# Two-layer recurrent attention kernel: attend spread over four 64x64 tiles, q's feature rows reordered, last transposes one expert later

## The chip, the core and the metric

The kernel runs on one core of one Trainium2 chip. A core has five engines that run in parallel, each with its own queue of instructions in a fixed order: TensorE (PE; its weight loads are shown as PEld), VectorE (DVE), ScalarE (ACT), GpSimd (POOL) and SyncE (SP, which here only issues DMAs). An instruction at the head of a queue that has to wait holds everything behind it on that engine. The metric is the device time of one execution in microseconds; lower is better.

## What is computed

Two layers of attention multiplied by a gated feed-forward network, on `x` of 4 x 512 x 128 in float32. The change is in the first attention and in the feature rows of the second. The first attention (16 heads, key and value width 64, segments of 64 tokens, a memory carried from segment to segment) is, cut to what matters:

```python
scores = einsum('bhid,bhjd->bhij', q, k) * scale        # own keys, causal mask
att_dot = einsum('bhij,bhjv->bhiv', softmax(scores), v)
sq = elu(q) + 1;  sk = elu(k) + 1
att_mem = sq @ M / (sq @ Z.T)
M_new = M + einsum('bhld,bhlv->bhdv', sk, v);  Z_new = Z + sk.sum(-2)
att = gate * att_mem + (1 - gate) * att_dot              # gate = sigmoid(betas)
out = att.reshape(B, 64, H * DV) @ Wo
```

The result `x + out * silu(ffn(xn))` is normalised and goes through a second attention (16 heads of width 8, 16 channels, softmax over 512 keys) and a second network of 8 experts. The second attention is computed through features: a product of pairs of elements of q gives part of the softmax's denominators.

## The kernel before, in words

**Stages.** The order of the program is: layer norm and the first network (0 to about 92 us of the profile, `norm_ffn0`), the first attention (`attn0`, 92 to 354), the experts of the second network (`ffn1`, about 349 to 490), and the second attention (`attn1`, 490 to the end). Nearly all instructions go through helpers that pin them in the order in which they are written (`mm1` L311 for matmuls, `act1` L314 for ScalarE, `dma1` L323 for SP's DMAs), so the lines of the profile are often those of helpers and the tiles' names tell what an instruction is. Memsets, POOL's products of the first attention and its loads are not pinned; a scheduler puts them where their inputs are ready.

**First attention.** `attn0` works through 32 segments n, 8 for each of 4 batches. A segment has 16 heads, laid out as 4 x 2 x 2 by hp, a and p: head number 4*hp + 2*a + p. Matmuls use 64x64 corners of PE: the rows of a corner are set by the half of the partitions (0 to 63 or 64 to 127, `halves`) in which the operands lie, its columns by the half in which the result lies. In the loop L816 to L856, segment n does in this order on PE: `scores(n+1)` (tile sc), chunks of the projection of a later group (pp for q and k, pv for v; `todo`, three a segment), with `memory(n)` (mm: queries on the memory) and `update(n)` (mu: new memory) between them, `keys(n+1)` (pk: transposes of the keys), then `attend(n)` (dot: softmax weights on the values), in whose middle the transposes of `attended(n-1)` (pa) stand. Every fourth segment brings `output` (po: product with Wo). A dictionary `between` adds steps of the second network's normalisation to segments 18 to 24 and 30.5.

Each step leaves through other engines. VectorE: E from sc (L636), elu (L659), the division of mm and dot (L696, L697), the sum into the memory mz (L733), sums of keys (L664), and rd and sums0 for dot (L755, L757). ScalarE: exponentials (elu, up, E), copies out of PSUM (pj, vt, sk, attT). POOL: t1 by the gate (L714), t2 by one minus the gate (L762), their sum (L763), which pa then transposes. PSUM has three buffers of two banks (`wide`: sc, mm, mu, dot, po) and two of one bank (`narrow`: pp, pv, pk, pa), each used in turn.

In `memory` before the change, the result of head (hp, a, p) lies in half a; in `attend` too, and its operands E and v lie in half a as well (their partitions are the keys, and for keys the half is a). So a group of attend has only corners with equal row and column half. Its two turns go over hp in {0, 1} and {2, 3}, the turn with the transposes between. `attended` moves four transposes to the tile attT with one ScalarE copy of 128x512.

**The gate.** `load_first` loads betas with four DMAs on POOL's queue (L147) into `gate`, laid out as the result of attend is: half a, then hp, p. These come before POOL's setup of the first network in `begin0` (pick at L332 to L341, parts at L347).

**Experts.** `ffn1` goes over batches b and experts e: `up(b, e)` (ph, ScalarE's gelu h), then what `between` holds for (b, e), then `down` of the expert before (eo, added up on VectorE, L957 and L959). `left` holds what the first attention has left: `attended(31)` and `output(7)`. `begin` allocates and fills the second attention's tiles (memsets on POOL, L1150 and L1154) and makes the list of preparations, of which eleven follow from step 13 on.

**Second attention.** `attn1` goes over 64 steps i, 16 for each batch (t = i % 16): each step has 24 matmuls into acc from three functions of the scores, four score matmuls s, two steps ahead, and one preparation or mixing step. ScalarE makes two of the three functions and VectorE the third (L1548). The work for the next batch is spread over t by `prepare1`: tokens k at t = 0 (POOL: tokk, feat, L1207 to L1210), k and q at t = 2 and 3 (POOL splits them into three bf16 parts, L1254 and L1257; SP stores the parts into kd and qd, and q into qe and qf), feature sums pl at t = 4, 7, 9, 11. Every fourth step, `operands1` loads the next group's k and q from kd and qd. `features1` loads the rows of the features (6 DMAs rows from qe, 10 other from qf), and its two `products` multiply rows by other on POOL (L1321). There is one tile `rows` for each half mm of the heads and one tile `other` for both. `bank1` reads the products at t = 8 and 15. The step in which a load is issued and those in which its products stand are the numbers of the table L1617 to L1623.

Of the kernel before, what the change touches and what calls it, by code (L numbers as in the profile page):

```python
# [95 lines left out]
class Kernel:  # L96
# [9 lines left out]
    def load_first(self, pool, pool_attn):  # L106
# [37 lines left out]
        for p in range(2):  # L144
            for a in range(2):

                nc.gpsimd.dma_start(  # L147
                    out=self.gate[a * 64 : a * 64 + 64, :, p, :],
                    in_=be[a, p].partition_broadcast(64),
                )  # L150
# [392 lines left out]
    def attn0(self, xnT, g0, stack, psum, between):  # L543
# [155 lines left out]
        def memory(n):  # L699

            mz, sq = self.mz[(n % 8 + 1) % 2 + 1 if n % 8 else 0], seg[n][0]
            ps = wide(f"mm{n}")
            for hp in range(4):
                for p in range(2):
                    for a in range(2):
                        self.mm1(
                            ps[halves[a], p, hp * (DK + 1) : (hp + 1) * (DK + 1)],
                            lhsT=sq[halves[p], 2 * hp + a, :], rhs=mz[halves[p], hp, a, :],
                            start=True, stop=True,
                        )  # L710
            t = seg[n]["t1"] = pool.tile([P, 4, 2, DK], F32, name=f"t1{n}", tag="t1")
            r = pool.tile([P, 2, 4], F32, name=f"rm{n}", tag="rm")
            divided(ps, t.rearrange("p hp y d -> p y hp d"), r, heads(ps)[:, :, :, DK])
            nc.gpsimd.tensor_mul(t, t, self.gate)  # L714
# [22 lines left out]
        def attend(n, between):  # L737
# [4 lines left out]
            for turn in range(2):  # L742
                for hp in range(2):
                    for p in range(2):
                        for a in range(2):
                            bank, at = (turn + a) % 2, (hp * 2 + p) * (DK + 1)
                            self.mm1(
                                ps[halves[a], bank, at : at + DK + 1],
                                lhsT=e[halves[a], p, bank * 2 + hp, :],
                                rhs=v[halves[a], bank * 2 + hp, p, :], start=True, stop=True,  # L750
                            )
                if turn == 0:
                    between()
# [12 lines left out]
        def attended(n):  # L766

            if n % 4 == 0:

                attT[n // 4] = pool.tile([P, 16, 4, 32], F32, name=f"attT{n}", tag="attT")  # L770
            ps = narrow(f"pa{n}").rearrange("p (hp c) -> p hp c", hp=4)
            for hp in range(4):
                self.pin(nc.tensor.transpose(
                    ps[:, hp, :], seg[n]["att"][:, hp].rearrange("i p v -> i (p v)"),
                    self.ident,
                ))
            self.act1(
                attT[n // 4][:, :, n % 4],
                ps.rearrange("p hp (x c) -> p c (hp x)", c=16), AF.Copy,
            )  # L780
# [35 lines left out]
        for n in range(nseg):  # L816
# [33 lines left out]
            if more and n:  # L850
# [3 lines left out]
            attend(n, (lambda: attended(n - 1)) if n else (lambda: keys(1)))  # L854
# [704 lines left out]
    def attn1(self, xnT, g1):  # L1559
# [4 lines left out]
        with tc.tile_pool(name="a1", bufs=2) as self.a1, tc.tile_pool(  # L1564
# [44 lines left out]
            n = B * 16  # L1609
# [5 lines left out]
            for fb in range(B):  # L1615
                at = fb * 16
                for mm, load, make in (  # L1617
                    (0, at - 7 if fb else 1, at - 4 if fb else 3),
                    (1, at + (1 if fb else 5), at + (6 if fb else 8)),
                ):  # L1620
                    loads.setdefault(load, []).append((fb, mm))
                    for half in range(2):
                        makes.setdefault(make + half, []).append((fb, mm, half))  # L1623
# [342 lines left out]
    def run(self):  # L1966
# [15 lines left out]
        with tc.tile_pool(name="wf1", bufs=1) as wf1, tc.tile_pool(name="f1", bufs=1) as f1:  # L1982
            stack = ExitStack()
            w0 = stack.enter_context(tc.tile_pool(name="w0", bufs=1))
            with tc.tile_pool(name="wf0", bufs=1) as wf0:
                self.load_first(wf0, w0)
# [3 lines left out]
            with tc.tile_pool(name="ap", bufs=1, space=PSUM) as psum:  # L1990
# [23 lines left out]
                def prepare():  # L2014
# [5 lines left out]
                    (0, 1): [(left[0],)], (0, 2): [(left[1],), (begin,)], (0, 3): [(first.sums, 2)],  # L2020
# [77 lines left out]
```

## Time and profile before

| what | value |
|---|---|
| median of 3 runs | 818.4 us (818.02 to 820.14) |
| the profiled execution | 816.52 us, of which the span of the trace is 814.8 us |
| PE busy | 770.7 us (95%) |
| VectorE busy | 594.9 us (73%) |
| ScalarE busy | 505.7 us (62%) |
| POOL busy | 406.9 us (50%) |
| granted clock of PE, mean | 0.985 |

Times in the profile are microseconds from the start of the span, except that the mean of one instruction is in nanoseconds. A group is given as line, engine, operation, result <- inputs with their shapes, count; then busy time and mean; then the idle time of the engine before these instructions and what ended it. A float32 matmul leaves two records, so the 16 x 32 matmuls of attend stand as x1024. In a timeline the bracket at the end of a line is idle time of the engine ahead of it and the instruction that ended it. Busy times of one group are the time in which at least one of its instructions runs, so matmuls that overlap are not counted twice.

### The profile page before, as it was taken

Reading aid. Unit: us, or ns where it says so; the run is one execution under the profiler, and the core shown is the slowest. Engines: PE = TensorE matmul, PEld = TensorE weight load, DVE = VectorE, ACT = ScalarE, POOL = GpSimd, SP = SyncE. Lnnn points to the kernel's source line nnn. Section 1 sums busy time; section 2 is a strip of 40 time slices with the busy share of each in tenths; the row PEclk is TensorE's granted clock in tenths of the full one; section 3 lists DMA queues with packets and bytes.
Section 4 is the critical chain, followed back from the end, with each engine's and each line's share of the span. In section 5 each row is a group of like instructions: output and inputs, shape, how many; then the busy total and the mean of one; then the engine's idle time right before and its main releaser. Section 6 shows DMA issues by size and latency. Waiting matters only on the chain. (4 is left out here: it accounts for less than half of the span.)

```text
span 814.8 us, 23068 instructions
## 1 busy us (share of the span) xinstructions
PE 770.7 (95%) x9708; PEld 452.6 (56%) x9708; DVE 594.9 (73%) x1126; ACT 505.7 (62%) x692; POOL 406.9 (50%) x430
## 2 busy tenths in 40 slices
PE   8999899999999999789999999994999999999996
PEld 4566578787787777666777773331334333422325
DVE  7774687877779779825443338894998999898784
ACT  4333576766767657434432249993897889799760
POOL 7850055646555435545051006937697489624321
PEclk9999999999999999999999999997999999999999
DMA  8700522312313121000015003252344135322000
GB/s 216 170 16 1 155 64 61 93 41 81 92 29 93 29 80 29 16 2 1 1 39 182 1 1 104 87 174 84 107 160 123 41 111 162 105 59 65 1 15 17
DMA packets 74478, 59.21 MB, mean 73 GB/s; under 512 B 41264, under 2 KB 66128, under 8 KB 72928
## 3 DMA queue, kind: packets, MB, share of 16 engines
q1 hardware_dynamic: 72176, 56.25, 23.5%
q0 software_dynamic: 1616, 1.16, 0.9%
q8 instruction: 78, 1.28, 0.7%
q10 hardware_dynamic: 576, 0.26, 0.1%
q14 instruction: 32, 0.26, 0.1%
HBM read 36.41 MB, written 20.97 MB: 70 GB/s over the span
## 5 line engine op out<-in xcount | busy, mean ns | idle before, releaser
L1548 DVE TENSOR_TENSOR e<-e,e 128x1024 f32<-128x1024 f32 x126 | 200.9, 1633 | 15.1 <-ACT e L314 14.8
L311 PE MATMUL acc<-e,strip 128*32 128x512 f32 x1520 | 186.3, 599 | 1.6 <-DVE e L1548 1.5
L314 ACT ACTIVATE e<-s 128x1024 f32<-128x1024 f32 x126 | 122.5, 1029 | 47.9 <-PE s L311 47.6
L314 ACT ACTIVATE e<-e 128x1024 f32<-128x1024 f32 x126 | 127.0, 1070 | 0.0
L311 PEld LDWEIGHTS acc<-e,strip 128*32 128x32 f32 x1520 | 45.9, 109 | 117.2 <-issue 95.1
L314 ACT ACTIVATE h<-ph 128x1024 f32<-128x1024 f32 x32 | 32.8, 1024 | 87.0 <-PE ph L311 87.0
L1321 POOL TENSOR_TENSOR rows<-rows,other 128x512 f32<-128x512 f32 x32 | 62.6, 1985 | 25.1 <-DMA other<-qf 18.1
L659 DVE SCALAR_TENSOR_TENSOR elu<-elu,up 128x512 f32<-128x512 f32 x60 | 68.2, 1137 | 8.5 <-ACT up L314 8.4
L762 POOL TENSOR_TENSOR t<-t,gate 128x512 f32<-128x512 f32 x32 | 40.8, 1275 | 57.3 <-DVE t L697 45.7
L959 DVE SCALAR_TENSOR_TENSOR g<-eo,gw,g 128x128 f32<-128x128 f32 x112 | 31.5, 344 | 49.5 <-PE eo L311 49.5
L311 PEld LDWEIGHTS eo<-w_out,h 128*128 128x128 f32 x512 | 60.9, 192 | 11.7 <-issue 10.4
L314 ACT ACTIVATE pj<-pp 128x512 f32<-128x512 f32 x64 | 38.1, 596 | 44.2 <-PE pp L311 43.8
L311 PE MATMUL eo<-w_out,h 128*128 128x128 f32 x512 | 63.2, 277 | 1.0 <-DVE g L959 0.8
L311 PE MATMUL ph<-xnT,w_in 128*128 128x512 f32 x128 | 61.0, 599 | 0.0
L714 POOL TENSOR_TENSOR t<-t,gate 128x512 f32<-128x512 f32 x32 | 41.2, 1287 | 26.2 <-DVE t L697 26.2
L311 PE MATMUL s<-q,k 64*128 64x512 bf16 x256 | 39.2, 385 | 12.0 <-DMA q<-qd 10.7
L763 POOL TENSOR_TENSOR t<-t,t 128x512 f32<-128x512 f32 x32 | 45.8, 1430 | 2.5
L1207 POOL COPY tokk<-tokk 128x512 f32<-128x512 f32 x4 | 2.4, 610 | 88.8 <-DVE tokk L1196 88.8
L311 PE MATMUL dot<-vone,E 64*64 64x65 f32 x1024 | 44.8, 227 | 0.0
L311 PEld LDWEIGHTS <-k 64*128 64x128 bf16 x256 | 7.4, 94 | 64.9 <-issue 50.0
L311 PEld LDWEIGHTS dot<-vone,E 64*64 64x64 f32 x1024 | 35.8, 137 | 12.2 <-issue 10.9
L314 ACT ACTIVATE elu<-pj 128x512 f32<-128x512 f32 x60 | 37.3, 622 | 0.1
(277 smaller groups left out, 1475.3 us busy)
## 6 DMA issues: line engine op xcount, KB each, us to landing
vd<-vt SPq DMA_DIRECT2D x32, 256.0 KB
vone<-vd SPq DMA_DIRECT2D x64, 128.0 KB
rows<-qe SPq DMA_DIRECT2D x48, 128.0 KB
other<-qf SPq DMA_DIRECT2D x80, 64.0 KB
k<-kd SPq DMA_DIRECT2D x16, 256.0 KB
q<-qd SPq DMA_DIRECT2D x16, 256.0 KB
kd<-partk SPq DMA_DIRECT2D x12, 256.0 KB
qd<-partq SPq DMA_DIRECT2D x12, 256.0 KB
```

The lines of the kernel that those rows point to most:

```text
L311: return self.pin(self.nc.tensor.matmul(*args, **kw))
L314: return self.pin(self.nc.scalar.activation(*args, **kw))
L659: self.vec1(nc.vector.scalar_tensor_tensor(t, t, 1.0, up, ALU.min, ALU.add))
L714: nc.gpsimd.tensor_mul(t, t, self.gate)
L762: nc.gpsimd.tensor_mul(t, t, gate2)
L763: nc.gpsimd.tensor_add(t, t, seg[n]["t1"])
L959: self.vec1(v.scalar_tensor_tensor(acc[b][:, k, :], eo[:, k, :], w, acc[b][:, k, :], ALU.mult, ALU.add))
L1207: self.pool1(nc.gpsimd.tensor_copy(twice[:, :, D1 : 2 * D1], t))
L1321: self.pool1(nc.gpsimd.tensor_mul(rows[:, r], rows[:, r], other[:, r]))
L1548: self.vec1(self.nc.vector.tensor_mul(t, src[0][pair], src[1][pair]))
```

## The change

Five things are changed.

1. `memory` and `attend` write the result of head (hp, a, p) to half (a + hp) % 2, that is crossed for odd hp. In attend, a group of four matmuls now has all four corners, and the bank of a result is a, its row half. The result's place within the bank changes with it (2*u + p in attend, 2*a + hp // 2 in memory, in units of 65). The outputs are stored in the same shapes as before.
2. The gate's layout follows: eight DMAs of half the size in place of four (`crossed`). The fallback branch loads with `crossed` false, also by eight DMAs.
3. `attended` puts its transposes behind all of attend's matmuls, and copies them by four ScalarE copies of 128x128 in place of one of 128x512, since each pair (h, a) goes to other columns of attT. For segment 1, `keys` stands ahead of attend too.
4. In the second attention, the rows for mm = 0 of a batch after the first are loaded at step 16*b - 5 (was - 7) and multiplied at - 2 and - 1 (were - 4 and - 3); for the first batch both halves of mm = 0 are multiplied at step 3 (were 3 and 4), and those of mm = 1 are loaded at 4 (was 5) and multiplied at 6 and 7 (were 8 and 9).
5. In the experts of batch 0, `sums` of batch 2 comes at expert 1 (was 3), `attended(31)` at 2 (was 1), `output(7)` and `begin` at 3 (were at 2).

On SP, by the two programs' orders, the second feature loads of the first batch now stand before the stores of qe, qf and qd, and the loads of k and q at step 10 before the next batch's feature loads. On POOL, all four products of mm = 0 stand before the parts of k.

```diff
-    def load_first(self, pool, pool_attn):
+    def load_first(self, pool, pool_attn, crossed=False):
...
-                nc.gpsimd.dma_start(
-                    out=self.gate[a * 64 : a * 64 + 64, :, p, :],
-                    in_=be[a, p].partition_broadcast(64),
-                )
+                for x in range(2):
+                    rows, cols = (a, slice(x, 4, 2))
+                    if crossed:
+                        rows, cols = (a + x) % 2, slice(2 * a, 2 * a + 2)
+                    nc.gpsimd.dma_start(
+                        out=self.gate[rows * 64 : rows * 64 + 64, cols, p, :],
+                        in_=be[a, p, x:4:2].partition_broadcast(64),
+                    )
...
                     for a in range(2):
+                        at = (2 * a + hp // 2) * (DK + 1)
                         self.mm1(
-                            ps[halves[a], p, hp * (DK + 1) : (hp + 1) * (DK + 1)],
+                            ps[halves[(a + hp) % 2], p, at : at + DK + 1],
                             lhsT=sq[halves[p], 2 * hp + a, :], rhs=mz[halves[p], hp, a, :],
...
-        def attend(n, between):
+        def attend(n):
...
-            for turn in range(2):
-                for hp in range(2):
-                    for p in range(2):
+            for u in range(2):
+                for p in range(2):
+                    for hp in (2 * u, 2 * u + 1):
                         for a in range(2):
-                            bank, at = (turn + a) % 2, (hp * 2 + p) * (DK + 1)
+                            at = (2 * u + p) * (DK + 1)
                             self.mm1(
-                                ps[halves[a], bank, at : at + DK + 1],
-                                lhsT=e[halves[a], p, bank * 2 + hp, :],
-                                rhs=v[halves[a], bank * 2 + hp, p, :], start=True, stop=True,
+                                ps[halves[(a + hp) % 2], a, at : at + DK + 1],
+                                lhsT=e[halves[a], p, hp, :], rhs=v[halves[a], hp, p, :],
+                                start=True, stop=True,
                             )
-                if turn == 0:
-                    between()
...
-            self.act1(
-                attT[n // 4][:, :, n % 4],
-                ps.rearrange("p hp (x c) -> p c (hp x)", c=16), AF.Copy,
-            )
+            src = ps.rearrange("p (a u) (h t c) -> p c a u h t", a=2, h=2, c=16)
+            dst = attT[n // 4][:, :, n % 4].rearrange("p c (u y t) -> p c u y t", u=2, y=4)
+            for h in range(2):
+                for a in range(2):
+                    self.act1(dst[:, :, :, (a + h) % 2 * 2 + a], src[:, :, a, :, h], AF.Copy)
...
-            if more and n:
+            if more:
                 keys(n + 1)
...
-            attend(n, (lambda: attended(n - 1)) if n else (lambda: keys(1)))
+            attend(n)
+            if n:
+                attended(n - 1)
...
-                    (0, at - 7 if fb else 1, at - 4 if fb else 3),
-                    (1, at + (1 if fb else 5), at + (6 if fb else 8)),
+                    (0, at - 5 if fb else 1, (at - 2, at - 1) if fb else (3, 3)),
+                    (1, at + (1 if fb else 4), (at + 6, at + 7)),
                 ):
                     loads.setdefault(load, []).append((fb, mm))
                     for half in range(2):
-                        makes.setdefault(make + half, []).append((fb, mm, half))
+                        makes.setdefault(make[half], []).append((fb, mm, half))
...
-                self.load_first(wf0, w0)
+                self.load_first(wf0, w0, True)
...
-                    (0, 1): [(left[0],)], (0, 2): [(left[1],), (begin,)], (0, 3): [(first.sums, 2)],
+                    (0, 1): [(first.sums, 2)], (0, 2): [(left[0],)], (0, 3): [(left[1],), (begin,)],
```

## The prediction

> **What bounds the kernel now.** I read the busy time by stretches first, then the groups of instructions, then timelines of the places found. Columns of the stretches: length, busy us of each engine with its instructions, granted clock, DMA.
>
> ```profile
> core 0: us, PE busy (x) PEld busy (x) DVE busy (x) ACT busy (x) POOL busy (x), PEclk, DMA share, GB/s
> 100.00:250.00 150.00, 149.26 (x3426) 118.18 (x3424) 115.25 (x231) 101.60 (x183) 82.61 (x76) 1.00 0.25 70
> 250.00:320.00 70.00, 66.92 (x1421) 52.50 (x1424) 56.96 (x150) 48.45 (x84) 32.03 (x31) 0.98 0.20 56
> 320.00:354.00 34.00, 26.79 (x651) 21.66 (x644) 25.35 (x54) 16.52 (x28) 21.72 (x19) 0.90 0.08 18
> 553.60:564.40 10.80, 0.14 (x6) 0.10 (x4) 2.64 (x2) 0.15 (x1) 5.99 (x4) 0.73 0.49 143
> ```
>
> The first attention (about 92 to 354) is PE's: 149.26 of 150 us up to 250, with VectorE at 77% and ScalarE at 68%. Towards its end, where no projection is left to fill PE, other engines' latency rules. In the second attention PE stands still for over 10 us at 553.6. So PE time counts in 100 to 250, waits count in the tail, and one stall is a separate matter.
>
> ```profile
> L311 PE MATMUL dot<-vone,E 64*64 64x65 f32 x1024 | 44.8, 227 | 0.0
> L311 PE MATMUL mm<-mz,elu 64*64 64x65 f32 x1024 | 23.1, 227 | 0.1
> L659 DVE SCALAR_TENSOR_TENSOR elu<-elu,up 128x512 f32<-128x512 f32 x60 | 68.2, 1137 | 8.5 <-ACT up L314 8.4
> ```
>
> Two groups of the same count, tile and mean duration, one with twice the busy time: "dot" (attend) has two matmuls in flight at once, "mm" (memory) four. The third line is for the danger on VectorE: this operation takes 0.68 us alone and up to 1.48 us beside POOL.
>
> In order of time on PE (start, length; the last column counts):
>
> ```profile
> 299.59 0.68 PE L311 MATMUL dot<-vone,E 64*64 64x65 f32 x16
> 300.20 0.66 PE L773 MATMUL pa<-ident,t 128*128 128x128 f32 x4
> 300.79 0.62 PE L311 MATMUL dot<-vone,E 64*64 64x65 f32 x13
> ...
> 301.30 0.64 PE L311 MATMUL sc<-pj,pj 64*64 64x64 f32 x30
> 301.87 3.84 PE L311 MATMUL po<-l0wo,attT 64*128 64x128 f32 x64
> ```
>
> From the first dot to the end of sc it takes 301.87-299.59 = 2.28 us; starts count, since lengths overlap.
>
> The stall, SP's queue first:
>
> ```profile
> 528.75 3.77 SPq L323 DMA_DIRECT2D qd<-partq  x5
> 532.56 0.56 SPq L323 DMA_DIRECT2D rows<-other  x1
> ...
> 553.54 6.24 SPq L323 DMA_DIRECT2D other<-qf  x10
> ...
> 560.34 0.47 SPq L323 DMA_DIRECT2D q<-qd  x1
> ```
>
> then POOL, then PE:
>
> ```profile
> 545.49 8.02 POOL L1321 TENSOR_TENSOR rows<-rows,other 128x512 f32<-128x512 f32 x4 [13.36 <-DMA other<-qf]
> ```
>
> ```profile
> 564.33 1.04 PE L311 MATMUL s<-q,k 64*128 64x512 bf16 x4 [10.66 <-DMA q<-qd]
> ```
>
> Batch 0's second feature loads stand behind the qd stores (532.5), so their products end at 553.5. Only then is the tile "other" free for batch 1's loads, and the q that PE needs stands behind these on SP, though its data was stored at 532.5.
>
> **What the Trainium skill says.** TensorEngine Tiling (Array Packing), Tiling Modes: 64x64 mode has four independent tiles; a change of mode drains the array. The two groups agree (44.8 against 23.1). SBUF — State Buffer, SBUF: two separate sides: VectorE and GpSimd share a port pair as an exclusive lock; 0.68 to 1.48 us in L659 agrees. DMA: Bandwidth & Descriptors, Anatomy of one DMA — SWDGE (gpsimd) path: waits are taken on the issuing sequencer before dispatch; so a waiting DMA holds all behind it, as at 553.54. TensorE: Matmul & The Clock Gate, Part 1: after an idle window the array runs at half speed; behind the stall s takes 1.04 us, not 0.60.
>
> **The change part by part.**
>
> *Four tiles in attend, transposes after it.* All 32 dot records now run as mm does: 0.63 us from start to next start (313.85 to 314.48). After: 0.63 dot + 0.59 pa + 0.63 sc = 1.85, so 0.43 to 0.44 us saved a segment. Bounds: nothing, if two row halves meet in one bank (the new index puts each half in its own bank, so I exclude a loss), and 0.68, the difference of busy sums over 32. 26 segments lie in 100 to 320: 18 before 250 at 0.44 give 7.9; 8 after it, where VectorE has the segment hooks, I count at half, 1.8. The five of the tail: 27 and 28 are VectorE's (back to back from 320.2 to 333.2), worth 0.4 for both; at 346.51 and 352.62 pa waits 1.34 and 0.31 for POOL with half a dot behind it, which now goes first, 1.7. Sum 11.8. The new columns of memory cost nothing: the same four tiles, order within a group changed.
>
> *Four ScalarE copies for one.* No 128x128 ScalarE copy is in the trace; between 0.20 (128x4) and 0.60 (128x512) each. ScalarE: Activation LUTs, What ACT_TABLE_LOAD costs, prices 186 ns + 0.833 N, overlapping by 93: 0.61 for 512 (trace 0.597) and 0.89 for four of 128. So 0.3 us more on ScalarE, 9.6 in all, on an engine at 68%. PE meets the buffer two tiles later, some 2.3 us on; the cover is that, and 9.6 us is the price without it. Queued behind the copies are the next elu_exp pair, for VectorE's elu.
>
> *VectorE.* Its busy share goes from 77% to 81%; a full segment with both elu stretched takes it 6.7 us (321.00 to 327.72), PE afterwards 7.24-0.44 = 6.8. Idle before rd is 20.4 us over 25 segments, enough for 0.44 each. I charge 1.0 (0 to 6) for jitter.
>
> *Gate loads.* Four more DMA issues on POOL at 0.63 (L147: 2.51 for four) = 2.5 us ahead of everything. The memset of parts ends 11.9 and becomes 14.4; VectorE's cast at 13.06 and with it PE's rwt are late by 1.4. The pick cast is hidden behind that. Loss 1.4 (0 to 2.5).
>
> *Last steps one expert later.* pa of segment 31 waits 2.34 us at 358.14 for POOL; now an up and a down (3.6 us) go first: 2.3 won. The sums of batch 2 fall into VectorE's 5.28 us idle time before 360.63. Output 7, the x add and begin's memsets (3.5 + 2 x 2.8 on POOL) come one expert later, with no reader before the second batch of experts; the sums of batch 3 lose a step of cover, some 1.2 us on VectorE, hidden by two eo buffers.
>
> *Order of q's rows.* All four products of batch 0 go ahead of partk: done at 508.4+7.5 = 516; partk ends 525 instead of 520.6, partq at 532 as before. On SP: kd to 525.5, the second features (10.9 us) to 536.4, qe and qf (7.7) to 544.1, qd (3.1) to 547.2, then k and q of batch 1, no longer behind batch 1's features. With 2.3 for the store to land and 3.85 for q, it is there at 553.7 to 554.4, PE wants it at 553.67: 0.7 left of 10.66. The 2.0 us of half speed behind it (s 0.27, mix 0.92, acc 0.86, by starts) goes too. But a new wait comes: batch 1's features are issued 550.2 to 560.5, land at 563; products 8.0, pr adds 3.5, tokk and feat 10.5 follow on POOL to 585. PE wants feat for pl (now at 594.78; less 10.66-0.7+2.0 it is 582.8): about 2.2, and I take 3.0 (0 to 6). Net 10.66+2.0-0.7-3.0 = 9.0. Later batches have 7 us of slack there.
>
> Sum: 11.8+2.3+9.0-1.4-1.0 = 20.7 us. The profiled execution is 816.5 (span 814.8) and goes to 795.8; the median of the runs shown, 818.4, is 1.9 above it and goes to 797.7.
>
> **Rivals.** (B) The matmul gain is swallowed by VectorE at 6.7 us a segment or by POOL: only 2.3+9.0-1.4 remain, 808.5. For it, the tail; against it, 23% idle VectorE. (C) The stall only moves, to q itself or to feat: 818.4-11.7 = 806.7. For it, the 0.7 margin; against it, q's data is ready at 547. (D) Nothing is late next: no 0.7, 3.0, or 1.0, 793; with 0.68 a segment on the first 18, 788.7. (E) Slower: the strided copies cost far more. ScalarE has 4.6 us of other work a segment (nine starts, 0.50 to 0.53 apart), so four copies of c make 4.6+4c against 7.24 now; past c = 0.74 it eats all 9.9 that the rest wins. At 1.0, 27 segments lose 1.36 each: 845. Against it: 512 elements take 0.597 with a strided pattern today.
>
> **Numbers.** Likeliest (A) 797.7, own range 792 to 803: 0.56; B 0.12; C 0.13; D 0.15; E 0.04. The range of 789 to 808 leaves out E, half of B and little of D. A measurement of this kernel tells about 0.3% from no change; faster by more 0.95, within it 0.01, slower 0.04.
>
> **What would show it.** Right: dot's busy time near 23; dot to the end of sc 1.85; four attT copies at 0.28; no 2.34 wait of pa; at s of batch 1 a wait under 2; a wait of pl on feat some 3 us. Wrong: copies over 0.5, idle PE before mu or pk in 100 to 250, s waiting for q over 5, or products of batch 0 later than 520 from the same start.

## The result, and the profile after

The changed kernel takes 804.7 us (median of 4 runs, 803.49 to 806.29) against 818.2 us (817.18 to 820.14) for the kernel before on the same chip: a ratio of 0.9833, 95% interval 0.9808 to 0.9859. That is 13.5 us less, where 20.7 were predicted (797.7 us, range 789 to 808). The profiled execution takes 806.29 us with a span of 804.2 us, 10.6 us shorter than the span of before.

Comparing the starts of the same matmuls in the two traces, stage by stage, gives the account of those 10.6 us (positive: won):

| stage | predicted | measured |
|---|---|---|
| start, to the first sc | -1.4 | 91.83 - 94.38: -2.55 |
| first attention, first sc to first eo | 11.8 + 2.3 - 1.0 = 13.1 | 266.81 - 253.01: +13.80 |
| experts, first eo to the second attention | 0 | 131.40 - 134.29: -2.89 |
| second attention, to its last s | 9.0 | +1.5 |
| after the last s | 0 | +0.8 |

So the matmul part came out near its price, and the row part kept a sixth of what was promised. Two things have to be known to read the table. Of the 13.80 us, some 0.4 is the transposes of segment 31, which now stand behind the first eo (350.90 to 351.33) and so count in the next row; without this move the two rows are 13.4 and -2.5. And +1.5 is one profile: the same table of rows with the same attention won 2.5 to 3.2 us in the five other profiles of the experiments, little more than a third of 9.0 at most. The profiled execution is 1.6 us above the median of its runs; one slow eo, shown below, is of that size.

First the stretches of the changed kernel (length, busy time of each engine with its instructions, granted clock, DMA). The fourth is the one in which PE now passes the steps where it stood still before:

```profile
100.00:250.00 150.00, 146.82 (x3539) 113.43 (x3541) 111.53 (x245) 106.90 (x247) 85.00 (x81) 1.00 0.27 76
250.00:320.00 70.00, 63.69 (x1500) 49.80 (x1489) 59.99 (x154) 50.07 (x109) 34.83 (x33) 0.98 0.21 53
320.00:354.00 34.00, 27.62 (x523) 21.47 (x524) 24.56 (x58) 15.41 (x37) 19.94 (x17) 0.90 0.01 3
543.20:554.00 10.80, 10.80 (x102) 2.82 (x100) 9.82 (x12) 10.24 (x13) 0.27 (x1) 1.00 0.58 166
```

PE is still nearly full up to 250 (146.82 of 150 us), with more instructions in the same time. VectorE did not become the bound: 111.53 of 150 us. In the last stretch PE works for all of 10.80 us where it worked for 0.14.

The groups of instructions of the changed kernel:

```profile
L664 DVE SCALAR_TENSOR_TENSOR elu<-elu,up 128x512 f32<-128x512 f32 x60 | 56.4, 941 | 16.1 <-ACT up L319 15.9
L319 ACT ACTIVATE attT<-pa 128x128 f32<-128x128 f32 x128 | 25.1, 283 | 19.3 <-PE pa L778 19.3
L316 PE MATMUL mm<-mz,elu 64*64 64x65 f32 x1024 | 23.0, 227 | 0.9 <-DVE elu L664 0.9
L316 PE MATMUL dot<-vone,E 64*64 64x65 f32 x1024 | 22.7, 227 | 0.0
```

dot now costs what mm costs, at the same 227 ns a matmul: four in flight. The new copies take 283 ns each. elu got cheaper without being touched, 941 ns instead of 1137; the experiment with the transposes in the middle shows where that came from.

In time on PE, a segment of the changed kernel:

```profile
332.83 0.70 PE L316 MATMUL dot<-vone,E 64*64 64x65 f32 x32
333.45 0.66 PE L778 MATMUL pa<-ident,t 128*128 128x128 f32 x4
334.04 0.69 PE L316 MATMUL sc<-pj,pj 64*64 64x64 f32 x32
```

By starts, dot takes 0.62 and pa 0.59; with 0.63 for sc that is 1.84 against 2.28 before.

SP's queue at the former stall: q's store is issued at 535.14, the load of k follows at once and that of q at 541.88; no load that waits for POOL's products stands between.

```profile
535.14 3.18 SPq L328 DMA_DIRECT2D qd<-partq  x5
538.43 0.45 SPq L328 DMA_DIRECT2D k<-kd  x1
541.88 0.36 SPq L328 DMA_DIRECT2D q<-qd  x1
```

That is what the new order was predicted to do, and s no longer waits. But here is POOL from the landing of batch 1's first rows on:

```profile
554.44 9.03 POOL L1329 TENSOR_TENSOR rows<-rows,other 128x512 f32<-128x512 f32 x4 [10.97 <-DMA other<-qf]
563.41 3.50 POOL L1407 TENSOR_TENSOR pr<-pr,pr 128x512 f32<-128x512 f32 x2
566.85 1.61 POOL L1215 COPY tokk<-tokk 128x512 f32<-128x512 f32 x1
568.43 8.21 POOL L1217 TENSOR_TENSOR feat<-tokk 128x512 f32<-128x512 f32 x5
576.58 2.11 POOL L1218 COPY feat<-tokk 128x512 f32<-128x512 f32 x1
```

Each line starts where the last one ends. POOL idles 10.97 us for the rows, and then owes 24 us of work before feat is done at 578.7. PE, which is no longer held up, comes for feat earlier:

```profile
578.74 1.89 PE L316 MATMUL pl<-strip,feat 128*64 128x9 f32 x32 [3.55 <-POOL feat L1218]
580.55 4.48 PE L316 MATMUL acc<-e,strip 128*32 128x512 f32 x24
```

A wait of 3.55 us, and behind it acc takes 4.48 us where it takes 2.78 elsewhere. From the s of one step to that of the next it takes 10.38 us (574.58 to 584.96) in place of 4.29: 6.1 us lost, 3.55 of them the wait and 2.5 the slow pl and acc.

### The profile page after: what moved, and what is told of

The parts are those of the page before. It is cut to its first block, busy times and chain, and to the rows that moved or that the text cites. A ratio compares the mean times of both kernels' runs of the same rounds, so it can differ in the third digit from the quotient of the medians.

```text
span 804.2 us, 23193 instructions
## 1 busy us (share of the span) xinstructions
PE 760.7 (95%) x9708; PEld 439.7 (55%) x9708; DVE 586.9 (73%) x1126; ACT 509.4 (63%) x788; POOL 407.4 (51%) x434
## 5 line engine op out<-in xcount | busy, mean ns | idle before, releaser
L316 PE MATMUL acc<-e,strip 128*32 128x512 f32 x1520 | 190.6, 602 | 3.2 <-DVE e L1556 3.1
L664 DVE SCALAR_TENSOR_TENSOR elu<-elu,up 128x512 f32<-128x512 f32 x60 | 56.4, 941 | 16.1 <-ACT up L319 15.9
L1215 POOL COPY tokk<-tokk 128x512 f32<-128x512 f32 x4 | 4.3, 1076 | 77.2 <-DVE tokk L1204 77.2
L319 ACT ACTIVATE up<-pj 128x512 f32<-128x512 f32 x60 | 37.8, 630 | 0.0
L319 ACT ACTIVATE attT<-pa 128x128 f32<-128x128 f32 x128 | 25.1, 283 | 19.3 <-PE pa L778 19.3
```

Source lines behind the costliest of these rows:

```text
L316: return self.pin(self.nc.tensor.matmul(*args, **kw))
L319: return self.pin(self.nc.scalar.activation(*args, **kw))
L664: self.vec1(nc.vector.scalar_tensor_tensor(t, t, 1.0, up, ALU.min, ALU.add))
```

## The experiments

Each run is the kernel named with one edit. Times are medians; the ratio is to the kernel before on the same chip. The runs were on several chips, on which the kernel before took 818.0 to 820.0 us, so across rows the ratio is the safer number. The changed kernel stands at 804.7 us, 0.9833.

| run | us | ratio (95%) |
|---|---|---|
| rows only | 815.3 | 0.9955 (0.9933 to 0.9977) |
| old rows | 806.2 | 0.9863 (0.9837 to 0.9890) |
| feat first | 813.8 | 0.9951 (0.9936 to 0.9967) |
| feat first, products behind pr | 810.2 | 0.9887 (0.9866 to 0.9909) |
| table by batch | 803.5 | 0.9820 (0.9794 to 0.9845) |
| loads behind q | 802.9 | 0.9796 (0.9761 to 0.9831) |
| gate on SP | 802.2 | 0.9814 (0.9788 to 0.9840) |
| begin late | 803.2 | 0.9809 (0.9789 to 0.9829) |
| begin held | 803.0 | 0.9812 (0.9788 to 0.9836) |
| transposes in the middle | 806.9 | 0.9843 (0.9816 to 0.9869) |
| one copy | 802.8 | 0.9799 (0.9776 to 0.9821) |
| all together | 792.0 | 0.9653 (0.9627 to 0.9678) |

The intervals are some 2 us to either side, so differences of 1 to 2 us between runs are read from the traces, stage by stage. There too one has to know the scatter: the first attention, the same code in ten profiles, took 252.2 to 254.3 us (mean 253.1), and the first sc, with the gate loads on POOL, came at 93.4 to 95.6 us (mean 94.2 of ten).

In the second attention I count by the s matmuls: number n, counted from 0 to 63, is that of step n, issued two steps ahead of its use. "Ahead" means ahead of the kernel before at the same s.

**Rows only (rows_only), and everything but the rows (no_rows).** Part 4 alone on the kernel before, and the changed kernel with the old table. The diff is that of the first; the second undoes it.

```diff
-                    (0, at - 7 if fb else 1, at - 4 if fb else 3),
-                    (1, at + (1 if fb else 5), at + (6 if fb else 8)),
+                    (0, at - 5 if fb else 1, (at - 2, at - 1) if fb else (3, 3)),
+                    (1, at + (1 if fb else 4), (at + 6, at + 7)),
```

> The kernel before with the new order of q's rows alone. Theory: the order trades one wait for others. Read from the two traces, the second attention wins 12.9 us where s waited for q, and gives back 6.9 where pl waits for POOL's feat and then runs slowly, 0.7 beside the products and some 3.7 in the later batches; 1.6 us remain, so about 816.6 against 818.2 before. In the trace s waits under 1 us at the start of batch 1, pl between 3 and 4 us on feat some twenty steps after the start. Rival: the prediction's 9.0 us were right for the order by itself, and what was lost belongs to the way it meets the earlier stages: then about 809, and pl waits under 1 us.

> The changed kernel with the old order of q's rows. Theory: the second attention starts 8.4 us earlier than before the change and then runs as it did, stall of 10.7 us included: 818.2 - 8.4 = 809.8 us. Rival: the attention's gain is smaller than its trace shows and the rows brought most of the 13.5 us: then 813 or more.

Rows only: 815.3 against 818.0, and by the interval 2 to 5.5 us faster; the theory said 816.6, the rival 809. In its trace the stall gives 12.9 us (s number 15 to 17), and then pl waits 2.20 us for feat, and some steps on po waits for the additions of pr:

```profile
588.21 1.10 PE L311 MATMUL pl<-strip,feat 128*64 128x9 f32 x32 [2.20 <-POOL feat L1210]
612.38 0.49 PE L311 MATMUL po<-wo_rep,pr 128*128 128x128 f32 x2 [1.32 <-POOL pr L1399]
614.59 4.78 PE L311 MATMUL po<-wo_rep,pr 128*128 128x128 f32 x26 [1.72 <-POOL pr L1399]
```

po's step takes 13.23 us in place of 8.05. So the loss does not need the changed attention; only its place along POOL's chain differs. Old rows: 806.2, faster than the theory's 809.8, since its trace enters the second attention 11.0 us ahead of before, 2.7 more than the profile that the theory was drawn from. It leaves it 10.2 ahead, stall included. Within the second attention rows only wins 1.85 us, the changed kernel 1.5 (2.5 to 3.2 in the five later profiles with its table: gate on SP, begin late, begin held, transposes in the middle, one copy), old rows -0.9. Against old rows the new order is worth 2.4 to 4.1 us there, against the kernel before 1.5 to 3.2, not 9.0.

**Feat first (feat_first).** The products of the first rows of batches 1 to 3 behind tokk and feat, the second loads at step 4 of every batch.

```diff
-                    (0, at - 5 if fb else 1, (at - 2, at - 1) if fb else (3, 3)),
-                    (1, at + (1 if fb else 4), (at + 6, at + 7)),
+                    (0, at - 5 if fb else 1, (at + 2, at + 3) if fb else (3, 3)),
+                    (1, at + 4, (at + 6, at + 7)),
```

> The changed kernel, with the products of mm = 0 of the later batches multiplied after POOL's feat (steps at + 2 and at + 3) in place of before it, and the second loads at at + 4 for every batch. Theory: POOL then makes tokk and feat about 9 us earlier, pl finds them, and the 6.9 us lost there come back: about 798 us, down to 794 if the losses of the later batches come from the products beside VectorE's work at the turn of a batch. Rival: the products are only the first in a row; with them out of the way another wait takes the place, bank1 at step 8 for the products or q at step 10 for its store behind the second loads: then 802 us or more, and PE waits over 2 us there.

Measured 813.8: the theory held at pl, the rival on the time; the place of the new wait, po, neither had named. The same matmuls as shown above for the changed kernel, in this run:

```profile
574.51 1.11 PE L316 MATMUL pl<-strip,feat 128*64 128x9 f32 x32
575.55 2.94 PE L316 MATMUL acc<-e,strip 128*32 128x512 f32 x24
```

No wait, no slow acc; PE is 20.0 us ahead of the kernel before after that step, where the changed kernel is 13.5 ahead. Then it loses 9.0 us in one step, and 8.6 in the same step of the next batch:

```profile
603.68 0.80 PE L316 MATMUL po<-wo_rep,pr 128*128 128x128 f32 x2 [6.19 <-POOL pr L1407]
```

On POOL the second products (5.15 us from 597.26, idle 4.94 us for their loads) stand ahead of the additions of pr that po needs.

**Feat first with the products behind pr (feat2), and a table by batch (mixed).** First, the second products two steps later, at + 8 and at + 9. Then batch 1 so, and batches 2 and 3 with the old numbers.

```diff
-                    (1, at + 4, (at + 6, at + 7)),
+                    (1, at + 4, (at + 8, at + 9) if fb else (6, 7)),
```

```diff
+                    (0, *((1, (3, 3)), (11, (18, 19)), (25, (28, 29)), (41, (44, 45)))[fb]),
+                    (1, *((4, (6, 7)), (20, (24, 25)), (33, (38, 39)), (49, (54, 55)))[fb]),
```

> As the kernel with feat first, and the second products two steps later (at + 8 and at + 9), behind the additions of pr, for batches 1 to 3. In the trace of feat first the 6.9 us at pl are gone, but po waits 6.2 us and again 5.3 us a batch later for the additions of pr, which stand on POOL behind second products that wait for loads issued at 588 us. Theory: POOL's chain after the first loads of batch 1 is the bound, and only the order on it decides; with pr ahead of the second products po waits no longer, and the losses of 9.0 and 8.6 us there vanish: 813.8 - 17.6 = 796 us, PE about 20 us ahead of the kernel before from step 17 on. Rival: the chain is simply too long; bank1 at step 15 then waits for the second products, or q at step 10 for its store: over 803 us.

> Rows' table by batch: batch 0 as changed, batch 1 as in the kernel with feat first and second products at at + 8 and at + 9, batches 2 and 3 as in the kernel before the change. Theory: the small losses of the later batches in the changed trace (1.3 and 1.7 us in batch 2, 2.0 in batch 3) are POOL's products lying beside VectorE's e at the turn of a batch; in the old places they cost nothing, as the trace of the changed kernel with the old rows shows. So some 2 us better than feat2: about 795 us, no acc waiting for e in batches 2 and 3. Rival: these losses come from PE being earlier in the batch, not from the place of the products: then equal to feat2 within 1 us.

810.2 and 803.5, against 796 and 795: the wait of po went, and another took its place, the second of those that the rival had named for feat first. In the run with the products behind pr:

```profile
610.33 1.03 PE L316 MATMUL s<-q,k 64*128 64x512 bf16 x4 [7.04 <-DMA q<-qd]
611.29 3.48 PE L316 MATMUL den<-bank,to_den 128*64 128x512 f32 x8
```

and SP's queue ahead of it:

```profile
577.85 6.81 SPq L328 DMA_DIRECT2D kd<-partk  x5
584.76 3.67 SPq L328 DMA_DIRECT2D rows<-qe  x6
588.47 5.88 SPq L328 DMA_DIRECT2D other<-qf  x10
...
602.13 2.95 SPq L328 DMA_DIRECT2D qd<-partq  x5
605.17 0.45 SPq L328 DMA_DIRECT2D k<-kd  x1
```

The second loads hold SP for 9.6 us between k's store and q's, so q is stored at 602 and read at 605 to 608. The table by batch has the same wait (7.52 us). It settles the other question, though. Behind pl's wait, to the end of the second attention, the changed kernel loses 3.65 us net in its profile, the largest at s number 35 (1.25), 42 (1.24) and 51 (1.97), where PE waits for VectorE's e. (In the five other profiles with this table it is 1.9 to 4.3. The losses at 35 and 51 are in each of them; the one at 42 is in one of the five only, so it isn't the table's.) VectorE there, first the changed kernel, then the same pair with the old rows:

```profile
636.84 4.28 DVE L1556 TENSOR_TENSOR e<-e,e 128x1024 f32<-128x1024 f32 x2
```

```profile
640.56 2.34 DVE L1556 TENSOR_TENSOR e<-e,e 128x1024 f32<-128x1024 f32 x2
```

POOL adds pr beside the first pair (636.5 to 640.0), behind products that ended late, and is idle beside the second. With the old places for batches 2 and 3 the losses at 35 and 51 are gone: in the table by batch PE is 12.1 us ahead at s number 35 and 12.0 at the end.

**Loads behind q (mixed2).** Batch 1's second loads at step 26, behind the loads of k and q, and batch 2's first rows accordingly later.

```diff
+                    (0, *((1, (3, 3)), (11, (18, 19)), (28, (30, 31)), (41, (44, 45)))[fb]),
+                    (1, *((4, (6, 7)), (26, (27, 28)), (33, (38, 39)), (49, (54, 55)))[fb]),
```

> As mixed, with the second loads of batch 1 at step 26 behind the loads of k and q (were at 20, ahead of the stores of qe, qf and qd), their products at 27 and 28, and the first rows of batch 2 loaded at 28 and multiplied at 30 and 31. In mixed and feat2 s waits 7.5 and 7.0 us for q at step 26: SP issues the second loads for 9.6 us ahead of q's stores. Theory: with the loads behind, q is stored some 9 us earlier, the wait is gone, no other comes in its place, and of PE's lead 21.3 us before that step some 20 remain: 803.5 - 8 = 795.5 us. Rival: bank1 at step 31 now waits for the second products, which can't start before 608 us, or the first products of batch 2 lie beside VectorE's work at the turn of the batch: 800 us or more, with a wait over 4 us between steps 29 and 34.

802.9, with single runs from 796.3 to 805.9. In batch 1 the theory held: no wait, PE 18.6 us ahead from s number 23 to 34. Then batch 2 shows what batch 1 had shown under feat first: po waits for pr behind second products.

```profile
677.83 2.50 PE L316 MATMUL po<-wo_rep,pr 128*128 128x128 f32 x10 [1.11 <-POOL pr L1407]
```

2.9 us lost there; the second attention wins 7.3 us. Besides, the first attention of this profile was the longest of the ten (254.3), and from the last s to the end it took 31.1 us against 28.5 in the changed kernel, which was not followed. The expected 795.5 was not reached.

**Gate on SP (gate_sp).** The eight loads with `nc.sync.dma_start`, behind the weights.

> The changed kernel with the eight gate loads issued by SP after the weights instead of by POOL. Theory: the 4.7 us of issues on POOL hold up the memset of parts and through VectorE's casts the rwt matmuls; with them gone the first sc comes at 91.8 us or earlier in place of 94.4, and the time is 2.5 to 4 us less, 801 to 802. Rival: the start is bound by the loads of x and of the first network's weights, which arrived 0.9 us later in the changed trace for a reason of their own: then sc comes at 93.5 or later and the time falls by under 1 us.

802.2; the first sc comes at 92.88, 1.3 us before the mean of the others and 1.5 before the profile of the changed kernel, between theory and rival. The loads do cost: in the changed kernel POOL issues them from 4.63 to 9.37, the memset of parts ends at 14.16, and VectorE's parts hold PE. But taking them away uncovers another cost. POOL's setup of pick now runs from 5.36 to 8.96, beside VectorE's first xn, and the transposes come one by one, as the first two in this run show:

```profile
7.02 0.30 PE L399 MATMUL lnt<-ident,xn 128*128 128x128 f32 x1 [0.50 <-DVE xn L305]
7.67 0.33 PE L399 MATMUL lnt<-ident,xn 128*128 128x128 f32 x1 [0.34 <-DVE xn L305]
```

**Begin late (begin_late), and begin held (begin_later).** One batch of experts later, first by the table of steps alone, then with its memsets kept in order behind a copy of one element of batch 3's xnT.

```diff
-                    ... (0, 3): [(left[1],), (begin,)],
+                    ... (0, 3): [(left[1],)],
-                    (1, 0): [(first.hidden, 3)],
+                    (1, 0): [(first.hidden, 3), (begin,)],
```

```diff
+        tick = keep.tile([P, 1], F32, name="tick")
+        self.pool1(nc.gpsimd.tensor_copy(tick, done[:, 0, 0:1]))
-        nc.gpsimd.memset(self.feat, 1.0)
+        self.pool1(nc.gpsimd.memset(self.feat, 1.0))
```

> The changed kernel with begin one batch of experts later, at expert 0 of batch 1. Theory: its memsets on POOL then no longer lie beside VectorE's xn of batch 2, which in the changed trace took 2.9 us for four in place of 1.1 and held the transposes lnt for 1.6 us; 0.8 to 1.3 us come back on PE (more only where the slow clock behind that wait goes too): about 803.5, xn at 0.28 us each, no wait of lnt for xn. Rival: the wait only moves to other VectorE work of the experts beside the memsets, eo and its sums: then no change, or up to 1 us slower.

> The changed kernel with begin at expert 0 of batch 1, and its memsets kept in their order on POOL behind a copy of one element of xnT of batch 3. (In the kernel with begin late the memsets had not moved: they stood at 359.6 us as before, since nothing held them, so that run decides nothing.) Theory: without the memsets beside it VectorE makes the four xn in 1.1 us in place of 2.9, lnt waits no longer, and 0.7 to 0.9 us come back by the time that the second attention starts; the slow clock of the eo behind it, 1.5 us, which some runs have and others don't, goes too: lnt to eo in 1.9 us in place of 2.6. The time is 803 to 804. Rival: xn stays at 2.9 us, since it is slow for another reason (its place beside ScalarE's rstd and the eo sums): no change.

Moved by the table alone, the memsets stay at 359.6 (360.1 in the changed kernel): they have no input and no pinned place, and run when POOL comes to them. In all three kernels, the one before included, they follow at once on POOL's last sum of `output(7)`; that step moved by one expert, and they with it. The run is a second measurement of the changed kernel (803.2), and tells how far such repeats lie apart. Held, they start at 377. VectorE's four xn in the changed kernel and then in this one:

```profile
368.99 2.87 DVE L305 TENSOR_SCALAR xn<-x,mv,rstd 128x128 f32<-128x128 f32 x4
```

```profile
369.07 1.12 DVE L305 TENSOR_SCALAR xn<-x,mv,rstd 128x128 f32<-128x128 f32 x4
```

and what PE makes of it, again the changed kernel first:

```profile
371.91 0.33 PE L901 MATMUL lnt<-ident,xn 128*128 128x128 f32 x1 [1.61 <-DVE xn L305]
372.10 3.49 PE L316 MATMUL eo<-w_out,h 128*128 128x128 f32 x16
```

```profile
369.48 1.10 PE L901 MATMUL lnt<-ident,xn 128*128 128x128 f32 x4
371.37 2.02 PE L316 MATMUL eo<-w_out,h 128*128 128x128 f32 x16 [0.80 <-DVE g L967]
```

The wait for xn is gone, and from lnt to eo it takes 1.89 us, as before the change. The experts take 131.8 us here, 132.65 in the runs with the collision, and 134.3 in those with the collision and a slow eo (3.49 in place of 2.02). So the 2.89 us of the table come apart by the starts of eo: 0.44 for the transposes that moved, 0.81 for the collision, 1.64 for the slow eo. The slow eo is not tied to an edit: of ten profiles with the same wait of 1.61 us five had it. Nor is it new: in rows only the first eo takes 3.40 us behind the old wait of 2.34 us, and 1.95 behind the same wait in the kernel before. The theory held for the place and the size (0.8); the time of 803.0 is too close to the repeat's 803.2 to confirm it.

**Transposes in the middle (middle).** `attended(n - 1)` between the two pairs of heads of attend, all else as changed.

```diff
+                if u == 0 and between:
+                    between()
...
-            attend(n)
-            if n:
-                attended(n - 1)
+            attend(n, (lambda: attended(n - 1)) if n else None)
```

> The changed kernel with the transposes back in the middle of attend, between the two pairs of heads. It parts the gain of the four tiles from that of the later transposes. Theory: the four tiles bring it; two more changes of tile size a segment cost little, dot's busy time stays near 22.7, and only where pa waits for POOL in the tail half a dot now waits behind it: 1 to 2 us slower than the changed kernel, 806, the first sc to the first eo 254 to 255 us in place of 252.5 to 253.5. Rival: each change of tile size empties PE, and a good part of the 0.44 us a segment came from having fewer of them: 5 us slower or more.

806.9; the first sc to the first eo takes 256.2 us, 3.1 more than the mean of the ten: a little over the theory, well short of the rival. dot's busy time misses what the theory said, though:

```profile
L316 PE MATMUL dot<-vone,E 64*64 64x65 f32 x1024 | 30.1, 234 | 0.0
L664 DVE SCALAR_TENSOR_TENSOR elu<-elu,up 128x512 f32<-128x512 f32 x60 | 68.7, 1146 | 8.4 <-ACT up L319 8.3
```

64 half groups of 0.47 us overlap with their neighbours, so the sum of busy times is no price. By starts two more changes of tile size cost nothing: from the first dot to the end of sc a segment takes 1.84 us here (305.60 to 307.44), as undivided. Nor does the order lose anything while PE is full: at the 20th group of sc (of 31) this kernel is 6.9 us ahead of the kernel before, counted from the first sc, and the changed kernel 6.6. The difference comes behind it: to the last group of sc this kernel wins 1.1 us more and the changed kernel 3.2, and from there to the first eo 2.6 and 4.0. In that last piece half a dot stands behind a pa that waits 1.57 us for POOL, as the theory said; the rest was not followed to single waits. So of the 13.8 us some 10.7 belong to the tiles and what goes with them, and some 3 to the place of the transposes, from one profile of this kernel against ten that lie within 2.1 us. The second line shows that the cheaper elu comes from that place as well. VectorE was busy 121.7 us of 100 to 250 here and 111.5 in the changed kernel, with PE at 146.9 and 146.8 and nearly the same count of matmuls (3529 and 3539): ten us of VectorE more, and PE does the same work. VectorE is not the bound there.

**One copy (one_copy).** The old copy of 128x512, so that odd pairs of heads land in the wrong columns of attT.

> The changed kernel with one ScalarE copy of 128x512 for the transposes of a segment in place of four of 128x128; the output of odd pairs of heads then stands in the wrong columns of attT, so the attention's result is another. Theory: the copies cost 0.3 us of ScalarE a segment, hidden behind VectorE and PE: the same time within 1 us, 804.7. Rival: ScalarE is late for elu and up in many segments (VectorE's idle time before elu grew from 8.4 to 15.9 us in the changed trace), and the copies cost PE 3 us or more: under 802.

802.8, and the attention 251.6 us, just under the ten others. The cost of the copies can be read from PE. In the changed kernel po comes sooner behind the transposes whose copies it needs, and waits for these copies:

```profile
133.03 3.84 PE L316 MATMUL po<-l0wo,attT 64*128 64x128 f32 x64 [0.25 <-ACT attT L319]
```

There are six such waits of 0.25 us in the eight outputs; with one copy the six are 0.06 us each, and with the transposes in the middle, or before the change, there are none. So the four copies cost PE 6 x 0.19 = 1.1 us, a little over the theory and well short of the rival. On ScalarE they are busy 25.1 against 19.1 us: 6.0 more, where 9.6 was priced. Four in a row take 0.785 us from the first start to the last end, not the estimated 0.89.

**All together (combo).** The gate on SP, begin held, and the table of "loads behind q" with batch 2's second products at 40 and 41, behind the additions of pr.

> The changed kernel with the gate loads on SP, the memsets of begin held until after the transposes of batch 3, and the table of mixed2 with the second products of batch 2 two steps later (40 and 41), behind the additions of pr. (In mixed2 the wait of s for q was gone, but po waited for pr again, one batch on, and 2.9 us were lost.) Theory: the gains add up, since they lie in different stages. From the span of mixed2, 802.1: 2.9 for the po wait, 2.4 in the experts (131.8 us from the first eo to the second attention in place of 134.3), 1.5 at the start, and 1.1 because the first attention of that profile was 1.1 us longer than the mean of the runs with the same code: a span of 794, a time of 796. Rival: another wait on POOL's or SP's chain takes the place of the last one in batch 2 or 3: 800 us or more.

792.0 us (790.45 to 794.79), ratio 0.9653 (0.9627 to 0.9678): 28.0 us faster than before, 12.7 below the changed kernel's median on another chip, and 4 better than expected (2.6 of it behind the last s: 28.5 us, against the 31.1 of the profile from which the sum started). Its span is 789.9 us: first sc at 92.61, attention 253.2, experts 131.8, and the second attention wins 11.6 us over the one before, where the changed kernel won 1.5. No wait on feat, pr or q is left in it. The 12.9 us of the stall stay, less 0.7 at s number 7 and 0.8 at 22 and 23.

## Why the prediction was right, and where it failed

The time lies in the range of 789 to 808, but above the 792 to 803 of my own account; the range was wide enough to hold rival C's 806.7 too. That the number fell into it is no proof of the account: in the profile 10.6 of the 20.7 us came, and the second attention, priced at 9.0, gave 1.5.

**Right: the four tiles.** dot at 22.7 us (predicted near 23), dot to the end of sc 1.84 (1.85), the copies at 283 ns (0.28), and the 2.34 us for which pa of segment 31 waited for POOL gone with the new order of the last steps (part 5 has no run of its own). The two waits ahead of it stay: 1.34 and 1.62 us, before 1.34 and 0.31. Predicted 13.1, measured 13.8, or 13.4 without the transposes that moved. Some of this closeness is luck: by the starts of sc the 18 segments up to 250 won 6.75 us for 7.9, since po's wait for the copies was put at nothing, the next eight 2.9 for 1.8, and the 1.0 for jitter was not needed. The reading "20.4 us over 25 segments, enough for 0.44 each" was not sound: 4.6 of the 20.4 us lie in the last two segments and 7 of the 32 have none. It was not put to the test, since elu got cheaper. The rivals B (VectorE swallows it) and E (the copies cost far more) fall: VectorE at 111.5 of 150, copies at 0.28.

**Right in kind, too small: the gate loads.** -1.4 predicted (0 to 2.5), -2.3 to -2.6 measured. The issues took 4.74 us for eight, 2.2 more (2.5 assumed); rwt came 1.82 us later (16.47 for 14.65). The delay was not absorbed but passed on, and in the changed kernel's profile it grew by another wait for h, 0.75 us at 50. Not every repeat has that wait: begin late has none, and its first sc comes at 93.40.

**Failed: "Net 10.66+2.0-0.7-3.0 = 9.0".** Its first half came true (+12.85 for 12.0). Two terms fell. The wait of pl was taken at 3.0 and came at 3.55, but its price was 6.1 in this profile (5.3 to 6.5 behind the same wait in four others, 3.9 behind one of 2.19 us in begin held): I gave the half speed behind a wait to the stall that was removed (2.0) and not to the one that was put in. The granted clock in 578 to 586 is 0.62 in the changed kernel and 1.00 in the run with feat first. And "later batches have 7 us of slack there" looked at waits on POOL only: the products and the additions behind them, moved to the turn of the batch beside VectorE's e, cost 3.65 us in this profile (1.24 of it the loss at 42, which is not theirs), which the table by batch showed by taking the rest away. With 0.7 at s number 7, beside the four products of batch 0, and 0.8 just ahead of pl, 1.5 remain; that last 0.8, of which 0.6 is there without the wait too, was not followed.

The root is one: I treated the q stall as a wait of PE. It was the place where POOL's chain caught up. From the landing of batch 1's rows at 554 POOL has 48 us of work without a gap (products 9.0, pr 3.5, tokk and feat 11.9, the parts 11.4, second products 8.0, pr 4.5), and PE needs its results at three points. Remove PE's wait for q and PE meets the chain at pl; move feat ahead and it meets it at po; move pr ahead and it meets SP's queue at q; move the loads and only then is batch 1 free. Rival C ("the stall only moves, to q itself or to feat") named the mechanism and, at 806.7, lies nearer to 804.7 than my forecast does.

**Failed: "no reader before the second batch of experts".** True for data, and beside the point. The memsets of begin came one expert later and lay beside VectorE's xn. The section of the Trainium skill that I cited for the shared lock (SBUF — State Buffer, SBUF: two separate sides) says that a POOL instruction and certain VectorE instructions exclude each other for their whole length, and the four xn at 2.87 us in place of 1.12 fit that; I applied it to elu alone. Cost 0.8 us, and 1.6 more in the profile with a slow eo. Open: why the clock drops behind the same 1.61 us wait in five profiles of ten.

## What to carry to other kernels

Ahead of removing a wait, write out what the other engines have still to do by then, each queue in order with durations, and see where the freed engine meets it next; price a new wait with the slow clock that may come behind it (here up to 2.9 us behind 3.55). When work is moved on POOL, ask what VectorE does at that time, even if no data connects them, and check where an unpinned instruction really goes. When a chain on one queue is the bound, keep changing its order until the last of its consumers is free: with the six tables tried the second attention won 1.5, -7.2, -4.6, 2.2, 7.3 and 11.6 us, each in one profile; the first, repeated, gave 2.5 to 3.2.

## What the hardware showed that I had not expected

- A memset on POOL, which reads nothing, stretched VectorE's xn from 1.12 to 2.87 us for four, and POOL's selects did the same at the start (3.00 us). The pair e took 4.28 in place of 2.34 us beside POOL's additions of pr.
- Behind a wait of 3.55 us PE ran at a granted clock of 0.62 over 8 us: acc 4.48 in place of 2.78. Over the eo behind the same wait of 1.61 us it was 1.00 in five profiles and 0.53 to 0.61 in five (eo 2.02 us, or 3.14 to 3.65).
- A dot in two halves around the transposes has a busy time of 30.1 us and undivided 22.7, while from the first dot to the end of sc both take 1.84 us: the sum of busy times grew by 7.4 us where the starts show no loss.
